# GpSimd's items of the last layer in chains of their own, given out at chosen steps, and the late transpositions of x at steps 7 and 8

## The chip, the cores and the metric

The kernel runs on one core of one Trainium2 chip. Its time is what the device takes for one execution, in microseconds (us); a kernel is judged by the median of several executions. A core has a tensor engine (PE, which loads weights on a second row of the profile, PEld), a vector engine (DVE), a scalar engine (ACT), GpSimd (POOL) and SyncE (SP), whose queue issues nearly all DMAs here. Each engine works through its own queue in order; semaphores tie them together.

## The reference

A small graph network over 16 sequences `b` of 1024 nodes with 128 features, all with one adjacency matrix. Three layers are multi-head attention with a feed-forward part, and one last layer is a graph attention with one head:

```
# layers 0, 1, 2 (8 heads of 16)
scores = einsum(Q, K) / sqrt(16);  attn = softmax(where(adj == 0, -inf, scores))
x = layer_norm(h + attn @ V @ Wo + bo)
x = layer_norm(x + relu(x @ W1 + b1) @ W2 + b2)
# last layer
h = x @ W;  e = leaky_relu(s_i[:, None] + s_j[None, :])      # s_i = h @ a_src, s_j = h @ a_dst
att = softmax(where(adj == 0, -inf, e));  out = layer_norm(att @ h + x) * gamma + beta
```

Everything is in float32.

## The kernel before, in words

**Blocks and steps.** The work is cut into 48 blocks `m`, one for each pair of a sequence and a layer 0 to 2. The sequences go in groups of four ("panels" below): blocks 0 to 11 are the three layers of sequences 0 to 3, blocks 12 to 23 those of sequences 4 to 7, and so on; within a panel all four do layer 0, then layer 1, then layer 2. A block has 32 steps, numbered 0 to 31; the running number of a step is `n`, so that step 4 of block 14 is n = 452. In a step, `score_step` makes the scores of 128 keys with 512 queries for four heads: PE makes two tiles of 128x1024 (L545), and each is masked and exponentiated. One of them goes by ACT (exp, L553) and then POOL (multiplication by a 0/1 mask, L554), the other by DVE (an added mask, L557) and then ACT (L569). At the ten steps of `BOTH_ON_DVE` (3, 7, 8, 15, 23, 24, 26, 28, 30, 31) both go by DVE, and POOL has no multiplication. Four steps later (`AHEAD`), `av_step` multiplies the result by V on PE (L574).

**Pieces.** All other work is cut into pieces that are given out between the steps: the projections of the next block (`proj_tasks`), what follows the attention of an earlier block (`post_tasks`), the transposition of the next `x` (`transpose_x`), and the last layer of a finished sequence (`last_tasks`). Pieces stand in chains. A task is `(gap, function, tiles)`: it is due `gap` steps after its predecessor in the chain. `piece` gives out at most one piece without a `*` in a step, and any number of those with one (those hold no work of PE). `need` takes pieces out of their chains at once, due or not, until a mark is done; it is called where the next block cannot start without something. In `tiles`, `+x` claims one of the five buffers for a sequence's `x`, `-x` gives it back; `w` and `last` are counted in the same way (8 and 2).

**What sets the order on the engines.** The order on PE, ACT and SP is the order of the program. POOL and DVE are ordered by the framework's scheduler, and `tc.issue_after(behind["pool"])` puts an item behind POOL's latest mask multiplication. A buffer is waited for where its new user stands, in that engine's queue.

**A panel's end.** When a sequence has finished layer 2, its last layer runs as pieces inside the blocks that follow. `xt` transposes x on PE, `nodes` makes h and the exponentials of the two scores, `rows_gh` and `send_rows` split these into rows and send them by 16 small DMAs on SP into `g_rows` and `h_rows` (L756, L757). Eight times, `edges(v)` makes the edge scores of 128 nodes on PE from those rows (L769), DVE masks them (L774), and `aggregate(v)` multiplies by h on PE (L383, 32 columns at a time), adds x on DVE and gathers the statistics of the final norm. After `aggregate(3)` and `aggregate(7)`, `normalise` works on half of the rows on POOL (L433 to L441). POOL multiplies x by the second norm's gain and adds its bias in place before that (`by_rows`, two of 128x1024), and multiplies and adds the last gain and bias afterwards (`by_rows` for each half, 128x512, all L798). `store` sends a half by four DMAs on SP. Only then is the buffer of x free, and `fetch` of a sequence of the next panel can claim it (eight DMAs on SP, L167). In a block whose `x` was fetched too late for the usual transposition by DMA, PE transposes it in two pieces with the mark `xP` (L345); their steps stand in `AT["xP"]`. `stack` (step 24 for the heads 0 to 3 of the next block, step 1 for the heads 4 to 7 of the running one) lays out Q and K with 16 DMAs on SP (L530).

**After the last step** the chains that are left are given out in turns until they are empty: the last layers of the sequences 13, 14 and 15 ("the tail" below).

Of the kernel before, what the change touches and what calls it, by code (L numbers as in the profile page):

```python
# [30 lines left out]
FIRST = 1  # L31


AT = {"xP": (4, 6), "proj": (5, 7, 9, 11, 17, 19), "post": (13, 15, 17, 18, 21, 22, 22, 23, 24, 25, 27, 29, 31, 35, 38, 40)}
AT_V_LAST = (9, 11, 17, 19, 20, 21)
AT_FIRST = (12, 14, 16, 18, 20, 22)
T_AT = 22
STACK_AT = 24
AT_END = {3: (12, 21, 22, 24, 25, 26, 27, 28, 30, 31), 2: (8, 9, 13, 14, 15, 16, 17, 18, 20, 21)}
AHEAD = 4  # L40
BOTH_ON_DVE = (3, 7, 8, 15, 23, 24, 26, 28, 30, 31)
TILES = {"w": 8, "x": LANES + 1, "last": 2}
BLOCKED = -57344.0
# [76 lines left out]
def fast_path(ctx: ExitStack, tc: tile.TileContext, a: dict, out: bass.AP, flag):  # L120
    nc = tc.nc
# [4 lines left out]
    L = 3  # L126
# [12 lines left out]
    def bank():  # L139

        if head[0] or tail[0]:
            return slot()[:, :512]
        return psum.tile([P, 512], F32, tag="t", name="t", bufs=1)
# [197 lines left out]
    def transpose_half(dst, src, h, gain=None, bias=None):  # L341

        ps = bank()
        for t in range(4):
            nc.tensor.transpose(ps[:, t * P:(t + 1) * P], src[:, 4 * h + t, :], identf)  # L345
        dv, pv = dst.rearrange("p (j t e) -> p t j e", j=4, t=4), ps.rearrange("p (t j e) -> p t j e", j=4, t=4)
        with soon():
            if gain is None:
                nc.scalar.copy(dv, pv)
            else:  # L350
                nc.scalar.activation(dv, pv, AF.Identity, scale=gain, bias=bias)
# [72 lines left out]
    def normalise(n, ts):  # L424

        scalars(n, ts)
        subtract_scale(n, ts)
# [68 lines left out]
    def transpose_x(m, by_dma=True):  # L496
        b, l = blocks[m]
        x, xT = state["x", b], xt_tile("xT")
        state["xT", m] = xT
        if by_dma:  # L500
            put(moved(lambda: xT, lambda: x), ("xT", m))
        elif m == 0:
            for h in range(2):
                transpose_half(xT[:, h], x, h)
        else:
            put([(0, lambda: transpose_half(xT[:, 0], x, 0), ""), (0, lambda: transpose_half(xT[:, 1], x, 1), "")],
                ("xP", m), first=True)

        def scale():
            with tc.issue_after(behind["pool"]) if m else nullcontext():  # L510
                nc.gpsimd.tensor_mul(x, x, rows(W[l - 1]["ln2_g"]))

        def shift():
            with tc.issue_after(behind["pool"]) if m else nullcontext():
                nc.gpsimd.tensor_add(x, x, rows(W[l]["bo"]))
        if m:
            put(([(6, scale, "*")] if l else []) + [(2 if l else 6, shift, "*")], ("shifted", m))
        else:
            shift()

# [180 lines left out]
    def last_tasks(b):  # L701
# [3 lines left out]
        def xt(h):  # L705
            def run():
                w = W[L - 1]
                if h == 0:

                    s["col"] = work.tile([P, 4, NT], F32, tag="col", name="col", bufs=2)  # L710
                    s["hd"] = [work.tile([P, 4, D + 1], F32, tag="w", name="hd", bufs=TILES["w"]) for _ in range(2)]
                    s["n"] = with_stats(state["x", b])
                s["xT", h] = half_tile("xT")
                transpose_half(s["xT", h], state["x", b], h, w["ln2_gc"], w["ln2_bc"])
            return run

        def nodes(t0, t1):
            def run():
                col, ts = s["col"], slice(t0, t1)

                halves = [slice(max(t0, 4 * h), min(t1, 4 * h + 4)) for h in range(2)]
                halves = [(c, s["hd"][c.start // 4][:, c.start % 4:(c.stop - 1) % 4 + 1, :])
                          for c in halves if c.start < c.stop]
                ps = bank()
                for t in range(t0, t1):
                    by_columns(ps[:, (t - t0) * (D + 2):(t - t0 + 1) * (D + 2)],
                               s["xT", t // 4][:, t % 4 * P:(t % 4 + 1) * P], w_nodes)
                pv = ps[:, :(t1 - t0) * (D + 2)].rearrange("p (t d) -> p t d", d=D + 2)
                with soon():
                    nc.scalar.activation(col[:, 2, ts], pv[:, :, D + 1], AF.Exp, scale=NEG_SLOPE)  # L730
                    nc.scalar.activation(col[:, 0:2, ts].rearrange("p c t -> p t c"), pv[:, :, D:], AF.Exp,
                                         scale=1 - NEG_SLOPE)
                    for c, hd in halves:
                        nc.vector.tensor_mul(hd[:, :, :D], pv[:, c.start - t0:c.stop - t0, :D],
                                             col[:, 2, c, None].to_broadcast([P, c.stop - c.start, D]))
                for c, hd in halves:
                    nc.scalar.copy(hd[:, :, D], col[:, 2, c])
            return run
# [22 lines left out]
        def edges(v):  # L761
# [14 lines left out]
                                                   1.0, mask01[:, :, q:q + SLOT], op0=OP.max, op1=OP.mult)  # L776
            return run

        def aggregate(v):
            def run():  # L780
                e, ps = s["e", v], bank()
                for t in range(NT):
                    by_columns(ps[:, :D + 1], e[:, t, :], s["hd"][t // 4][:, t % 4, :], start=(t == 0), stop=(t == NT - 1))
                nc.vector.reciprocal(s["col"][:, 3, v:v + 1], ps[:, D:D + 1])
                nc.vector.scalar_tensor_tensor(s["n"][0][:, v, :], ps[:, :D], s["col"][:, 3, v:v + 1],
                                               state["x", b][:, v, :], op0=OP.mult, op1=OP.add)
                stats(s["n"], slice(v, v + 1))
                if v % 4 == 3:
                    with tc.issue_after(behind["pool"]):
                        normalise(s["n"], slice(v - 3, v + 1))  # L790
                if v == NT - 1:
                    check_range(s["col"].rearrange("p c t -> p (c t)"))
            return run

        def by_rows(op, z, v, n=NT):
            def run():
                with tc.issue_after(behind["pool"]):
                    op(z(), z(), rows(v(), n))  # L798
            return run
# [16 lines left out]
        def two(f, g):  # L816
            def run():
# [1 line left out]
                g()  # L819
            return run  # L820

        mul, add = nc.gpsimd.tensor_mul, nc.gpsimd.tensor_add
        tasks = [(5, xt(0), "+w +last +w +w"), (1, xt(1), "+w"), (2, nodes(0, 3), ""), (2, nodes(3, 6), ""),
                 (0, by_rows(mul, x, lambda: W[L - 1]["ln2_g"]), "*"), (2, nodes(6, 8), "-w -w"),
                 (0, by_rows(add, x, lambda: ln2_b_last), "*"), (2, rows_gh, ""), (1, send_rows, "*"), (7, edges(0), "")]
        for v in range(NT - 1):
            tasks.append((2, two(edges(v + 1), aggregate(v)), ""))
            if v in (4, 6):
                tasks.append((0, by_rows((mul, add)[v // 2 - 2], y(0), lambda v=v: wl[("ln_gamma", "ln_beta")[v // 2 - 2]], 4), "*"))
        tasks += [(2, aggregate(NT - 1), ""), (2, store(0), "-last -w -w *"), (1, by_rows(mul, y(1), lambda: wl["ln_gamma"], 4), "*"),  # L830
                  (2, by_rows(add, y(1), lambda: wl["ln_beta"], 4), "*"), (3, store(1), "-x *")]
        return tasks


    blocks = [(b, l) for p in range(0, B, LANES) for l in range(L) for b in range(p, p + LANES)]
    chains = []
    done = {("fetch", b) for b in range(2)}
    now = [0]
    free = dict(TILES)
    free["x"] -= 2  # L840

    def put(tasks, mark, chain=None, first=False, table=None):

        if chain is None:
            chain = {"due": now[0], "queue": deque()}
            chains.insert(0 if first else len(chains), chain)
        for n, task in enumerate(tasks):
            at = now[0] // (4 * NT) * 4 * NT + (table or AT[mark[0]])[n] if mark[0] in AT else None
            chain["queue"].append(task + (mark if n == len(tasks) - 1 else None, at))
        return chain  # L850

    def take(chain):

        _, f, tiles, mark, _ = chain["queue"][0]
        if any(free[t[1:]] == 0 for t in tiles.split() if t[0] == "+"):
            return False
        chain["queue"].popleft()
        f()
        for t in tiles.replace("*", "").split():
            free[t[1:]] += -1 if t[0] == "+" else 1  # L860
        done.add(mark)
        chain["due"] = now[0]
        if not chain["queue"]:
            chains.remove(chain)
        return True

    def is_due(chain):
        gap, at = chain["queue"][0][0], chain["queue"][0][4]
        return now[0] >= max(chain["due"] + gap, at or 0)

    def piece():
# [371 lines left out]
```

## Time and profile before

| | |
|---|---|
| median of 3 runs | 3924.72 us (3922.28 to 3926.63) |
| profiled execution, its own time | 3922.55 us |
| its span in the profile | 3920.7 us |
| PE busy | 3715.7 us, 95% |
| POOL busy | 3477.6 us, 89% |
| DVE busy | 3460.5 us, 88% |
| ACT busy | 3296.9 us, 84% |
| issues of `h_rows` and `g_rows` on SP | 124 and 124 |
| score multiplications with the mask on POOL (L554) | 1056, 2029 ns each |
| a `by_rows` of 128x1024 and of 128x512 on POOL (L798) | 2392 ns and 1286 ns |

The span reaches from the first instruction to the last; some 2 us lie around it. A line of the timeline gives the start in us from the span's start, the duration, the engine and the source line, what is written and read, how many instructions are merged, and in brackets the idle time ahead of it and what ended it. "SPq" are DMA issues on SP. A line of the waits gives the waiting engine and line, the one that ended the wait, and the sum, the number and the longest of these waits. A line of the table by stage gives a stretch, its length, and the busy time of PE, PEld, DVE, ACT and POOL in it.

### The profile page before, as it was taken

To read this page: it belongs to the slowest core of one execution; us is meant where nothing else is said; L and a number is where in the kernel's file an instruction comes from. 1 tells how busy PE (TensorE), PEld (TensorE's weight loads), DVE (VectorE), ACT (ScalarE), POOL (GpSimd) and SP (SyncE) were. 2 spreads that over 40 slices of the span, in tenths; PEclk is the share of its full clock that TensorE was granted. 3 is DMA by queue.
4 is the path that set the end of the run, shared out by engine and by line. 5 is a ranking of instruction groups with operands and counts; after the bars stand their busy time and mean duration, and the time that the engine had idled before them with its cause. 6 is when DMAs were issued, how large, how long until landed. Compare 5 with 4: busy or idle time off the path is not lost.

```text
span 3920.7 us, 109674 instructions
## 1 busy us (share of the span) xinstructions
PE 3715.7 (95%) x44385; PEld 1515.1 (39%) x44385; DVE 3460.5 (88%) x5860; ACT 3296.9 (84%) x3797; POOL 3477.6 (89%) x2971
## 2 busy tenths in 40 slices
PE   7999999999989999999998999999999999999987
PEld 2333333344434333334443333333444433333346
DVE  6999999989878999998897899998898889999876
ACT  7989999977877999997777899999777789999850
POOL 5899999988978999998878899999887899999885
PEclk8999999999999999999999999999999999999998
DMA  5424334322323334332222324334232323424200
GB/s 139 113 73 103 91 81 110 76 70 70 89 63 79 98 72 110 80 95 73 72 67 76 92 66 101 95 74 100 73 82 52 88 71 93 103 71 106 63 8 21
DMA packets 245887, 319.28 MB, mean 81 GB/s; under 512 B 51072, under 2 KB 174208, under 8 KB 245376
## 3 DMA queue, kind: packets, MB, share of 16 engines
q1 hardware_dynamic: 243840, 311.52, 31.7%
q8 instruction: 353, 5.78, 0.6%
q14 instruction: 158, 1.29, 0.1%
q10 hardware_dynamic: 1536, 0.68, 0.1%
HBM read 58.53 MB, written 51.38 MB: 28 GB/s over the span
## 4 chain that ended last, share of the span: by engine, by line
POOL 46%; PE 38%; ACT 5%; DVE 5%; issue 3%; SPq 2%; DMA 1%; DVEq 0%; ACTq 0%; POOLq 0%
POOL e L554 27%; PE acc L574 13%; PE t L383 12%; PE s L545 9%; POOL x L441 7%; POOL mv L435 4%; POOL x L632 4%; ACT e L553 3%; DVE e L557 3%; ACT e L569 2%; PE s L769 2%; POOL x L798 2%; PE s L383 1%; POOL A L589 1%; SPq L530 1%
## 5 line engine op out<-in xcount | busy, mean ns | idle before, releaser
L557 DVE TENSOR_TENSOR e<-s,mask_add 128x1024 f32<-128x1024 f32 x2016 | 2377.4, 1211 | 240.3 <-PE s L545 214.5
L554 POOL TENSOR_TENSOR e<-e,mask 128x1024 f32<-128x1024 f32 x1056 | 2120.1, 2029 | 241.6 <-ACT e L553 227.8
L569 ACT ACTIVATE e<-e 128x1024 f32<-128x1024 f32 x2016 | 2110.9, 1062 | 185.2 <-DVE e L557 156.3
L574 PE MATMUL acc<-e,v 128*17 128x512 f32 x12288 | 1629.0, 602 | 78.6 <-POOL e L554 64.8
L553 ACT ACTIVATE e<-s 128x1024 f32<-128x1024 f32 x1056 | 1083.3, 1026 | 250.6 <-PE s L545 244.8
L545 PE MATMUL s<-Wq,Wk 64*128 64x512 f32 x6144 | 1196.4, 458 | 32.3 <-DVE e L557 21.1
L545 PEld LDWEIGHTS s<-Wq,Wk 64*128 64x128 f32 x6144 | 499.8, 185 | 1085.2 <-issue 388.9
L574 PEld LDWEIGHTS acc<-e,v 128*17 128x17 f32 x12288 | 205.2, 96 | 595.2 <-issue 351.1
L441 POOL TENSOR_SCALAR x<-x,mv 128x128 f32<-128x128 f32 x896 | 388.1, 448 | 19.1
L435 POOL TENSOR_TENSOR mv<-mv,half_neg 128x4 f32<-128x4 f32 (+1 forms) x179 | 214.0, 1195 | 13.6
L413 DVE BATCH_NORM_STATS2 st<-x 128x6 f32<-128x128 f32 x896 | 204.0, 281 | 7.7
L383 PE MATMUL t<-hd,ee 128*32 128x129 f32 x6656 | 205.7, 275 | 2.5 <-DVE x L420 2.4
L383 PE MATMUL t<-x1T,W 128*32 128x512 f32 x1520 | 201.9, 603 | 0.3
L774 DVE SCALAR_TENSOR_TENSOR ee<-s,mask 128x256 f32<-128x256 f32 x512 | 179.8, 413 | 23.4 <-PE s L769 23.4
L383 PEld LDWEIGHTS t<-W,hT 128*32 128x32 f32 x6080 | 170.9, 111 | 59.5 <-issue 48.4
L383 PEld LDWEIGHTS t<-hd,ee 128*32 128x32 f32 x6656 | 178.8, 110 | 16.1 <-DVE x L420 5.8
L383 PE MATMUL t<-W,hT 128*32 128x128 f32 x6080 | 184.7, 274 | 0.1
L589 POOL TENSOR_TENSOR A<-tt,recs 128x256 f32<-128x256 f32 x192 | 119.8, 624 | 49.7 <-DVE recs L588 49.6
L420 DVE TENSOR_TENSOR x<-t,x 128x512 f32<-128x512 f32 x191 | 129.1, 676 | 38.3 <-PE t L383 38.0
L649 ACT ACTIVATE hT<-t,b 128x512 f32<-128x512 f32 x190 | 130.4, 686 | 23.3 <-PE t L383 22.5
L585 DVE STREAM_TRANSPOSE tt<-acc 128x512 f32<-128x512 f32 x192 | 135.3, 705 | 0.0
L357 DVE STREAM_TRANSPOSE xb<-x 128x512 f32<-128x512 f32 x164 | 115.0, 701 | 20.1 <-POOL x L441 19.9
(145 smaller groups left out, 2531.1 us busy)
## 6 DMA issues: line engine op xcount, KB each, us to landing
Wk<-hi SPq DMA_DIRECT2D x384, 128.0 KB
Wk<-lo SPq DMA_DIRECT2D x384, 128.0 KB
Wq<-hi SPq DMA_DIRECT2D x384, 128.0 KB
Wq<-lo SPq DMA_DIRECT2D x384, 128.0 KB
tr<-xb SPq DMA_DIRECT2D x656, 64.0 KB
x1T<-tr SPq DMA_DIRECT2D x90, 256.0 KB
xT<-tr SPq DMA_DIRECT2D x74, 256.0 KB
x<-in_x_dram SPq DMA_DIRECT2D x124, 64.0 KB
```

The source lines that it names most:

```text
L383: nc.tensor.matmul(dst[j:j + SLOT, :], cols, rhs, start=start, stop=stop)
L413: nc.vector.bn_stats(st[:, t, :], z[:, t, :])
L435: nc.gpsimd.tensor_tensor(v, v, half_neg[:, ts], OP.pow)
L441: nc.gpsimd.tensor_scalar(z[:, t, :], z[:, t, :], mv[:, t, 0:1], mv[:, t, 1:2], op0=OP.add, op1=OP.mult)
L545: nc.tensor.matmul(ps[:, r * 512:(r + 1) * 512], k[64 * r:64 * r + 64, kt * P:(kt + 1) * P], q[64 * r:64 * r + 64, q0:q0 + 512], start=Tru ...
L553: nc.scalar.activation(ev, psv, AF.Exp, scale=HD ** -0.5)
L554: behind["pool"] = nc.gpsimd.tensor_mul(ev, ev, m).ins
L557: behind["dve"] = nc.vector.tensor_add(ev, psv, m).ins
L569: nc.scalar.activation(ev, ev, AF.Exp, scale=HD ** -0.5)
L574: nc.tensor.matmul(acc[j * SLOT:j * SLOT + HD + 1, :], v_bufs[m % 2][:, kt, 2 * j + g, :], e[:, j, :], start=first, stop=last)
L589: nc.gpsimd.tensor_mul(state["A"][:, qh, :, g, :], tt[:, :, :HD], rec[:, :, None].to_broadcast([P, 16, HD]))
L774: nc.vector.scalar_tensor_tensor(e[:, :, j * SLOT:(j + 1) * SLOT], ps.rearrange("p (k q) -> p k q", q=P)[:, :, j * SLOT:(j + 1) * SLOT], 1 ...
```

## The change

The items of POOL in the last layer leave the chain of the last layer. The two `by_rows` that scale x form a chain `("scaled", b)`, started by `xt(1)`; `aggregate` calls for it if it isn't done. `normalise`, the two `by_rows` of a half and its `store` form a chain `("out", b, h)`, started by `aggregate(3)` and continued by `aggregate(7)`. Tasks with a `~` are given out only at the steps of `POOL_FREE`, and two steps apart at the least, as long as no `need` takes them. The buffer of x and the count `last` are given back by the second `store`, the two `w` by `aggregate(7)`. `xP` moves from the steps 4 and 6 to 7 and 8, and `shift` of a layer 0 (adding a bias to x on POOL, 128x1024) from 6 to 10 steps after its chain's start.

```
-AT = {"xP": (4, 6), "proj": (5, 7, 9, 11, 17, 19), "post": (13, 15, 17, 18, 21, 22, 22, 23, 24, 25, 27, 29, 31, 35, 38, 40)}
+AT = {"xP": (7, 8), "proj": (5, 7, 9, 11, 17, 19), "post": (13, 15, 17, 18, 21, 22, 22, 23, 24, 25, 27, 29, 31, 35, 38, 40)}
+POOL_FREE = (0, 1, 2, 3, 4, 5, 6, 22, 23, 29, 30, 31)
...
-            put(([(6, scale, "*")] if l else []) + [(2 if l else 6, shift, "*")], ("shifted", m))
+            put(([(6, scale, "*")] if l else []) + [(2 if l else 10, shift, "*")], ("shifted", m))
...
                 transpose_half(s["xT", h], state["x", b], h, w["ln2_gc"], w["ln2_bc"])
+                if h == 1:
+                    put([(1, by_rows(mul, x, lambda: W[L - 1]["ln2_g"]), "*~"),
+                         (2, by_rows(add, x, lambda: ln2_b_last), "*~")], ("scaled", b), first=True)
...
+        def norm(h):
+            def run():
+                with tc.issue_after(behind["pool"]):
+                    normalise(s["n"], slice(4 * h, 4 * h + 4))
+            return run
         def aggregate(v):
             def run():
+                need_if(("scaled", b))
...
                 if v % 4 == 3:
-                    with tc.issue_after(behind["pool"]):
-                        normalise(s["n"], slice(v - 3, v + 1))
+                    s["out"] = put([(1, norm(v // 4), "*~"), (2, by_rows(mul, y(v // 4), lambda: wl["ln_gamma"], 4), "*~"),
+                         (1, by_rows(add, y(v // 4), lambda: wl["ln_beta"], 4), "*~"),
+                         (2, store(v // 4), "-x -last *" if v == NT - 1 else "*")], ("out", b, v // 4),
+                                   s["out"] if any(c is s.get("out") for c in chains) else None, first=True)
...
-                 (0, by_rows(mul, x, lambda: W[L - 1]["ln2_g"]), "*"), (2, nodes(6, 8), "-w -w"),
-                 (0, by_rows(add, x, lambda: ln2_b_last), "*"), (2, rows_gh, ""), (1, send_rows, "*"), (7, edges(0), "")]
+                 (2, nodes(6, 8), "-w -w"), (2, rows_gh, ""), (1, send_rows, "*"), (7, edges(0), "")]
         for v in range(NT - 1):
             tasks.append((2, two(edges(v + 1), aggregate(v)), ""))
-            if v in (4, 6):
-                tasks.append((0, by_rows((mul, add)[v // 2 - 2], y(0), lambda v=v: wl[("ln_gamma", "ln_beta")[v // 2 - 2]], 4), "*"))
-        tasks += [(2, aggregate(NT - 1), ""), (2, store(0), "-last -w -w *"), (1, by_rows(mul, y(1), lambda: wl["ln_gamma"], 4), "*"),
-                  (2, by_rows(add, y(1), lambda: wl["ln_beta"], 4), "*"), (3, store(1), "-x *")]
+        tasks.append((2, aggregate(NT - 1), "-w -w"))
...
     def take(chain):
...
+        if "~" in tiles:
+            pool_at[0] = now[0]
...
     def is_due(chain):
-        gap, at = chain["queue"][0][0], chain["queue"][0][4]
+        gap, tiles, at = chain["queue"][0][0], chain["queue"][0][2], chain["queue"][0][4]
+        if "~" in tiles and not tail[0] and (now[0] % (4 * NT) not in POOL_FREE or now[0] < pool_at[0] + 2):
+            return False
         return now[0] >= max(chain["due"] + gap, at or 0)
```

More of the change, by code (lines that the diff above doesn't have):

```diff
@@ L777, in edges @@
             return run
+        mul, add = nc.gpsimd.tensor_mul, nc.gpsimd.tensor_add
+        def norm(h):
[3 more added lines that the diff above has]
+            return run
         def aggregate(v):
             def run():
+                need_if(("scaled", b))
                 e, ps = s["e", v], bank()
@@ L820, in two @@
             return run
-        mul, add = nc.gpsimd.tensor_mul, nc.gpsimd.tensor_add
         tasks = [(5, xt(0), "+w +last +w +w"), (1, xt(1), "+w"), (2, nodes(0, 3), ""), (2, nodes(3, 6), ""),
-                 (0, by_rows(mul, x, lambda: W[L - 1]["ln2_g"]), "*"), (2, nodes(6, 8), "-w -w"),
-                 (0, by_rows(add, x, lambda: ln2_b_last), "*"), (2, rows_gh, ""), (1, send_rows, "*"), (7, edges(0), "")]
+                 (2, nodes(6, 8), "-w -w"), (2, rows_gh, ""), (1, send_rows, "*"), (7, edges(0), "")]
         for v in range(NT - 1):
             tasks.append((2, two(edges(v + 1), aggregate(v)), ""))
-            if v in (4, 6):
-                tasks.append((0, by_rows((mul, add)[v // 2 - 2], y(0), lambda v=v: wl[("ln_gamma", "ln_beta")[v // 2 - 2]], 4), "*"))
-        tasks += [(2, aggregate(NT - 1), ""), (2, store(0), "-last -w -w *"), (1, by_rows(mul, y(1), lambda: wl["ln_gamma"], 4), "*"),
-                  (2, by_rows(add, y(1), lambda: wl["ln_beta"], 4), "*"), (3, store(1), "-x *")]
+        tasks.append((2, aggregate(NT - 1), "-w -w"))
         return tasks
@@ L837, in fast_path @@
     done = {("fetch", b) for b in range(2)}
-    now = [0]
+    now, pool_at = [0], [0]
     free = dict(TILES)
@@ L858, in take @@
         f()
-        for t in tiles.replace("*", "").split():
+        if "~" in tiles:
+            pool_at[0] = now[0]
+        for t in tiles.replace("*", "").replace("~", "").split():
             free[t[1:]] += -1 if t[0] == "+" else 1
```

## The prediction

> **What bounds the kernel now.** I read the page's busy times first, then the busy times by stage, PE's waits in each stage, and the timelines of PE, POOL and SP where they differ.
>
> ```profile
> PE 3715.7 (95%) x44385; PEld 1515.1 (39%) x44385; DVE 3460.5 (88%) x5860; ACT 3296.9 (84%) x3797; POOL 3477.6 (89%) x2971
> ```
>
> PE is occupied nearly always, and the change leaves its work alone. So the change can only remove or add idle time of PE. The table by stage (a usual block, then 13 and 14) shows where that is:
>
> ```profile
> 392.10:462.50 70.40, 68.53 (x713) 24.14 (x707) 65.44 (x99) 67.18 (x75) 67.62 (x56) 1.00 0.39 92
> 1005.76:1098.15 92.39, 90.15 (x1333) 43.41 (x1329) 84.11 (x170) 70.26 (x85) 75.66 (x65) 1.00 0.25 66
> 1098.15:1196.31 98.16, 85.00 (x1086) 37.05 (x1083) 76.62 (x136) 71.56 (x89) 80.47 (x68) 0.97 0.30 78
> ```
>
> Block 14 idles for 13.2 us, the others for about 2. Its longest wait, and the tail's:
>
> ```profile
> 1117.58 1.08 PE L345 MATMUL t<-identf,x 128*128 128x128 f32 x4 [7.80 <-DMA x<-in_x_dram]
> 3857.55 1.08 PE L769 MATMUL s<-g_rows,h_rows 4*128 4x128 f32 x7 [5.21 <-DMA h_rows<-parts]
> ```
>
> The transposition of step 4 waits for a late `fetch`. PE's waits over the whole span have three of these, one for each panel but the last:
>
> ```profile
> PE t L345 <- DMA x<-in_x_dram: 21.0, 3, 7.8
> ```
>
> SP's timeline says why, in block 14 and then in block 13:
>
> ```profile
> 1090.31 20.66 SPq L812 DMA_DIRECT2D out_dram<-x  x8
> 1112.47 3.66 SPq L167 DMA_DIRECT2D x<-in_x_dram  x8
> ```
>
> ```profile
> 1002.47 4.81 SPq L167 DMA_DIRECT2D x<-in_x_dram  x8
> 1007.39 0.48 SPq L530 DMA_DIRECT2D Wk<-hi  x1
> ...
> 1016.79 1.23 SPq L530 DMA_DIRECT2D Wq<-lo  x2
> 1020.36 0.71 SPq L756 DMA_DIRECT2D g_rows<-parts  x1
> ...
> 1030.47 0.60 SPq L757 DMA_DIRECT2D h_rows<-parts  x1
> ```
>
> SP is one queue: `store`, `fetch`, `stack` (16 DMAs, 10.7 us) and `send_rows` (16 DMAs, 10.7 us) follow each other. In block 13 all of them are early enough: rows are usable about 1.5 us after the last issue (in block 23 it ended at 1780.2 and PE, waiting, went on at 1781.70), here at 1032.6, and the first `edges` needs them at 1038.78.
>
> ```profile
> 999.83 2.03 POOL L554 TENSOR_TENSOR e<-e,mask 128x1024 f32<-128x1024 f32 x1
> 1106.93 1.29 POOL L798 TENSOR_TENSOR x<-x,ln_beta 128x512 f32<-128x512 f32 x1
> ```
>
> From POOL's timeline: step 29's multiplication in block 12, and the last item of POOL ahead of block 14's `fetch`. It ends at 1108.2; the last store is issued 2.75 us later, `fetch` runs from 1112.47 to 1116.13, and PE uses x at 1117.58: 9.4 us from POOL's end to x, 7.9 to the end of `fetch` on SP.
>
> [...] nothing passes the 20.66 us above. [...] after 7.80 us of waiting four transpositions took 1.08 us instead of 0.66. Steps 4 to 7 of blocks 14, 26 and 38 last 18.5, 18.6 and 17.9 us against 9.2 in all for the same work (2.25 and 2.5 for steps 4 and 5 when they don't wait, then 2.2 and 2.3): a wait of 7 us costs 9.1 with its clock.
>
> **The change, part by part** (t = 0 is a block's first score; step lengths are distances of L545 in PE's timeline). From the order in which the changed program stands:
>
> *Block 14: -9.1 us.* `aggregate(7)` comes two steps earlier. Its PE work ends at about t = -3.5, DVE's statistics 2.2 us later, POOL's normalisation (3.5) and two `by_rows` (1.29 each, 1.36 with the gap) end at 4.9, and x is there at 14.3. The transpositions, now at steps 7 and 8, need it at 18. No wait remains.
>
> *Blocks 12 and 13: a burst.* The restriction to `POOL_FREE` leaves the items undone until block 12 (and 13) starts; there `need` for the next `fetch` takes all that is left, behind step 29's multiplication and ahead of step 0's. In block 12 this is a `by_rows` of x (2.39), two normalisations (3.5 each) and four halves (1.36 each): 14.8 us. Step 29's multiplication ends at -4.3, so the burst ends at 10.5 and step 0's multiplication at 12.5. PE wants that at step 4, t = 9.3: a wait of 3.2 us, +4 with some clock. The products of steps 1 and 2 follow at 14.5 and 16.5, and steps 5 and 6 ask at about 15 and 17, so they add little. x lands at 19.9, and step 7 asks at about 21.6. Behind `fetch` on SP stands `stack` for heads 4 to 7; it leaves at 10.5 + 7.9 + 10.7 = 29.1, and step 16 wants it at some 50: hidden. `send_rows` of this sequence went out before the burst, at step 29 of block 11.
>
> In block 13 it is two `by_rows` of x, one normalisation and four halves: 2.40 + 2.39 + 3.5 + 5.4 = 13.7 us from -5.0 to 8.7. `fetch` leaves SP at 8.7 + 7.9 = 16.6, 15 us later than today (1007.3, t = 1.5). Queued behind it are `stack` (to 27.4) and `send_rows` (to 38.2); the rows land at 39.7. Before, the first `edges` stood at step 14; it now stands at step 12, because `nodes` and `rows_gh` no longer make way for `xP`. The twelve steps last 27.2 us and `edges` comes 1.7 into its step: 28.9. PE waits 10.8 us in all (part of it already at step 0's product and at step 7 for x, at 18.1). With 2.1 for the clock, and 0.8 less for a wait at the block's end that `aggregate` no longer meets: +12.1.
>
> *Block 11, step 29: -3.3 us.* It lasts 5.1, 6.1 and 6.4 us in the panels, 2.8 without its wait for POOL; with step 30 that gives 2.3, 3.9 and 3.6. 11.7 us of POOL items leave the steps before it. The like wait in block 10 goes too, but its 2.3 to 3.9 us gain nothing: `edges(0)` at block 11's step 0 already waits for rows (2.0 us at 1781.70; at 822.77 it starts as they land), so PE only comes earlier to a queue that isn't faster.
>
> *Block 15: -2 us*: part of its idle excess over a usual block (1.4, 3.6 and 4.4), what waits for POOL.
>
> Sum for a panel: -9.1 + 4 + 12.1 - 3.3 - 2 = +1.7, three times +5. The later `shift` costs nothing: step 10 lies in stretches where PE paces the steps; at step 0 of blocks 1, 2 and 11 its 2.4 us fit before step 4.
>
> *Tail: +7 us.* In block 47 a 2.4 us wait for POOL goes, but 7.4 us of `by_rows` now stand between the last multiplication and the `by_rows` that the last feed-forward sum needs; the product `A` ends at 3815.8 instead of 3815.4, so this is even. Then SP: the first `store` of sequence 13 now stands ahead of `send_rows` of sequence 14. Its data need the fourth `aggregate` of sequence 13 (its PE work ends at 3842.1), POOL's two items for sequence 14 and a normalisation that stand ahead (to 3844.9), then a normalisation and two halves: ready at about 3851.1, gone from SP at 3853.5; 10.7 for the rows and 1.5 to land give 3865.8 instead of 3857.55: +8.2. The rows of sequence 15 get one more `aggregate` as cover: -1.1.
>
> Total +12.4 on the profiled execution's 3922.55 (span 3920.7, which I raise alike). That execution is 2.2 below the median of the runs, 3924.72, so I expect 3935 to 3937: **3936**.
>
> **Rivals.** *The rows are in time, so it is faster.* If `edges(0)` of block 13 finds its rows, all three panels lose 36 us less: 3912 by clearing two thirds of it, 3900 for all. For it: SP's chain is a sum of five parts that I take from other blocks, and POOL could reach the burst earlier than its multiplication of step 29 lets me think. Against it: `stack` takes 10.4 to 11.9 us wherever I look, `send_rows` 10.7 to 11.0, and POOL has nothing that it could put ahead. It decides at the lateness: below some 6.7 us instead of 10.8 the whole change gains. *The tail hides its store:* `norm` of sequence 13 done earlier, +5 in all, 3929; against it: that input, and what stands ahead of it on POOL. *POOL is later than I count:* the burst starts late or the blocks 14 and 15, where I find margins below 1 us, add waits: +4 a panel and more, 3950. *The change does nothing:* excluded, the orders on POOL, PE and SP differ.
>
> **How the numbers follow.** As computed 0.48 (own range 3925 to 3947), rows in time 0.24, tail hidden 0.15, POOL later 0.13. 0.2% (7.8 us) is about what a measurement tells from no change. Slower: 0.41 of the first, all of the last, a little of the third: 0.56. Faster: the rival and a bit of the first: 0.25. The range 3902 to 3952 takes in two fifths of the faster case.
>
> **What would show it.** Right: PE's L769 waits for `h_rows` or `g_rows` by about 10 us at step 12 of blocks 13, 25 and 37 and by about 12 in the tail; no L345 waits for x at block 14; L574 waits 3 us for POOL at step 4 of block 12. Wrong: `send_rows` of block 13 leaving SP before t = 30, or any of POOL's burst given out before step 29.

## The result, and the profile after

The changed kernel takes 3962.06 us (median of 4 runs, 3958.66 to 3964.19) against 3924.69 us before: a ratio of 1.0095 (1.0077 to 1.0112), slower. The forecast was 3936 with a range of 3902 to 3952: the direction is right, the loss is three times as large. The profiled span grew from 3920.7 to 3960.6 us.

Lines of the changed kernel lie some further down than before: scores L546, products with V L575, mask on POOL L555, `edges` L773, transposition L346, `fetch` L168, `store` L827. The busy times of the page after:

```profile
PE 3730.7 (94%) x44385; PEld 1519.2 (38%) x44385; DVE 3464.9 (87%) x5860; ACT 3295.5 (83%) x3797; POOL 3478.6 (88%) x2971
```

Each engine does the same work. PE is busy 15 us longer with as many instructions; more of them run at half clock (a granted clock of 0.50 in the trace, as from 1056.66 to 1061 us behind a wait of 4.70 us; the mean over the span is 0.978, and 0.983 before). The rest of the 40 us is idle time. The busy times by stage, for the blocks 12, 13 and 14:

```profile
919.12:1017.40 98.28, 93.37 (x1324) 44.07 (x1321) 82.71 (x164) 69.90 (x82) 82.40 (x78) 0.97 0.26 67
1017.40:1120.17 102.77, 92.40 (x1333) 44.49 (x1329) 83.59 (x167) 70.41 (x85) 80.95 (x77) 0.95 0.25 66
1120.17:1208.63 88.46, 83.10 (x1085) 36.14 (x1081) 77.27 (x140) 71.28 (x89) 79.58 (x66) 1.00 0.34 86
```

Block 14 is 9.7 us shorter than before, block 13 10.4 us longer, and block 12, where the forecast had 4, is 7.8 us longer. PE's waits show the exchange, first those of the kernel before for the rows and for `lo`, then those of the changed kernel:

```profile
PE t L383 <- DVE lo L473: 9.7, 6, 1.7
PE s L769 <- DMA h_rows<-parts: 6.3, 3, 5.2
...
PE s L769 <- DMA g_rows<-parts: 2.0, 1, 2.0
```

```profile
PE acc L575 <- POOL e L555: 64.3, 127, 3.6
PE s L773 <- DMA h_rows<-parts: 31.7, 7, 4.9
PE t L384 <- DVE lo L474: 18.0, 12, 2.2
PE s L773 <- DMA g_rows<-parts: 16.3, 4, 8.1
...
PE t L346 <- DMA x<-in_x_dram: 0.2, 1, 0.2
```

The 21.0 us for x have shrunk to 0.2; the waits for the rows grew from 8.3 to 48.0 us, and those for this `lo` on DVE (what `hi` leaves of a projection in layer 0) from 9.7 to 18.0, of which 6.6 are new waits at step 10 of blocks 12, 24 and 36. Block 13 shows what was forecast. SP's timeline, then PE's:

```profile
1020.66 8.10 SPq L827 DMA_DIRECT2D out_dram<-x  x8
1030.14 4.50 SPq L168 DMA_DIRECT2D x<-in_x_dram  x8
1034.74 0.48 SPq L531 DMA_DIRECT2D Wk<-hi  x1
...
1044.90 0.70 SPq L760 DMA_DIRECT2D g_rows<-parts  x1
...
1054.94 0.60 SPq L761 DMA_DIRECT2D h_rows<-parts  x1
```

```profile
1051.52 0.44 PE L773 MATMUL s<-g_rows,h_rows 4*128 4x128 f32 x1 [2.62 <-DMA g_rows<-parts]
1056.66 1.08 PE L773 MATMUL s<-g_rows,h_rows 4*128 4x128 f32 x7 [4.70 <-DMA h_rows<-parts]
```

`fetch` leaves SP 17.2 us into the block (forecast 16.6), the rows 38.1 (38.2), and PE goes on at 39.3 (39.7). It waits in two pieces, because the first of eight products needs fewer rows: 7.3 us in all (8.1 and 7.2 in blocks 25 and 37), where the prediction named about 10. The two other waits that it named are there too: 13 us for the rows in the tail (about 12 named), and 2.6 us for POOL at step 4 of block 12 (3 named).

The table gives the length of stages less that of the kernel before, in us, from the distances of the first score products; each sum is over the three panels. "Forecast" is the prediction's own working. Every column is one profiled execution, and not all are from one chip; the kernel before took 3923 to 3931 us on the chips of the experiments. The ratios below are each against it on the same chip, and they decide; the table says where.

| | forecast | after | e1 | e2 | e5 | e6 | e7 | e8 |
|---|---|---|---|---|---|---|---|---|
| block 2 | 0 | +5.2 | +0.1 | +4.2 | +5.1 | +0.2 | +0.1 | +4.4 |
| blocks 10, 11 | -9.9 | -3.5 | +0.9 | +0.3 | -1.0 | +0.5 | -4.1 | +2.1 |
| block 12 | +12 | +23.6 | +14.4 | +13.0 | +13.1 | 0.0 | +32.0 | +3.8 |
| block 13 | +36.3 | +34.6 | +13.8 | -7.9 | -6.7 | -6.7 | +26.7 | -6.7 |
| block 14 | -27.3 | -28.6 | -12.9 | -28.6 | -27.8 | -21.2 | -11.3 | -28.4 |
| block 15 | -6 | -1.7 | +0.2 | +0.4 | +0.4 | -0.5 | -0.2 | +0.1 |
| block 47 and tail | +7 | +11.5 | +2.1 | +9.3 | +3.2 | +1.5 | +10.7 | +0.9 |
| whole span | +12.4 | +39.9 | +20.2 | -8.0 | -12.1 | -24.8 | +55.9 | -24.1 |

### The profile page after: what moved, and what is told of

Read it like the earlier page. It is cut to its first block, busy times and chain, and to the rows that moved or that the text cites. A ratio compares the mean times of both kernels' runs of the same rounds, so it can differ in the third digit from the quotient of the medians.

```text
span 3960.6 us, 109707 instructions
## 1 busy us (share of the span) xinstructions
PE 3730.7 (94%) x44385; PEld 1519.2 (38%) x44385; DVE 3464.9 (87%) x5860; ACT 3295.5 (83%) x3797; POOL 3478.6 (88%) x2971
## 4 chain that ended last, share of the span: by engine, by line
POOL 46%; PE 37%; ACT 6%; DVE 3%; SPq 3%; issue 3%; DMA 2%; ACTq 0%; POOLq 0%; DVEq 0%
POOL e L555 27%; PE acc L575 13%; PE t L384 12%; PE s L546 9%; POOL x L442 7%; POOL mv L436 4%; POOL x L633 4%; ACT e L554 3%; ACT e L570 2%; POOL x L813 2%; PE s L773 2%; DVE e L558 2%; PE s L384 1%; SPq L531 1%; POOL A L590 1%
## 5 line engine op out<-in xcount | busy, mean ns | idle before, releaser
L555 POOL TENSOR_TENSOR e<-e,mask 128x1024 f32<-128x1024 f32 x1056 | 2119.1, 2027 | 284.4 <-ACT e L554 282.4
L575 PE MATMUL acc<-e,v 128*17 128x512 f32 x12288 | 1631.7, 603 | 73.6 <-POOL e L555 64.3
L546 PE MATMUL s<-Wq,Wk 64*128 64x512 f32 x6144 | 1201.0, 460 | 28.9 <-DVE e L558 15.6
L546 PEld LDWEIGHTS s<-Wq,Wk 64*128 64x128 f32 x6144 | 501.0, 186 | 1080.9 <-issue 386.7
L575 PEld LDWEIGHTS acc<-e,v 128*17 128x17 f32 x12288 | 204.7, 95 | 593.2 <-issue 354.3
L590 POOL TENSOR_TENSOR A<-tt,recs 128x256 f32<-128x256 f32 x192 | 119.6, 623 | 39.3 <-DVE recs L589 39.2
L650 ACT ACTIVATE hT<-t,b 128x512 f32<-128x512 f32 x190 | 130.4, 686 | 15.3 <-PE t L384 14.4
L773 PE MATMUL s<-g_rows,h_rows 4*128 4x128 f32 x1024 | 92.1, 296 | 48.3 <-DMA h_rows<-parts 31.7
```

Source lines behind the costliest of these rows:

```text
L546: nc.tensor.matmul(ps[:, r * 512:(r + 1) * 512], k[64 * r:64 * r + 64, kt * P:(kt + 1) * P], q[64 * r:64 * r + 64, q0:q0 + 512], start=Tru ...
L555: behind["pool"] = nc.gpsimd.tensor_mul(ev, ev, m).ins
L575: nc.tensor.matmul(acc[j * SLOT:j * SLOT + HD + 1, :], v_bufs[m % 2][:, kt, 2 * j + g, :], e[:, j, :], start=first, stop=last)
L773: nc.tensor.matmul(ps[:, r * 512 + k * P:r * 512 + (k + 1) * P], h_rows[row, k * P:(k + 1) * P], g_rows[row, half].rearrange("p (j q) -> p ...
```

## The experiments

**e1: the late transpositions alone, and what they need.**

```
# against the kernel before
-AT = {"xP": (4, 6), ...
+AT = {"xP": (7, 8), ...
```

> The kernel before with the late transpositions of x alone (xP at steps 7 and 8); POOL's items stay in the old chain and are given out as they fall due. Theory (the gain and the loss of the change are separable, and the loss is all in the chains): PE's wait for x at step 4 of blocks 14, 26 and 38 goes with its half clock, about 9.5 us each; the wait of 0.8 us at the end of blocks 13, 25 and 37 goes too, 2 to 3 us with its clock; nothing is added. 3924.7 - 3 x 12 = 3889, at most 3897 if block 13 keeps its wait. Rival (the late transpositions cost something by themselves: K's projection at step 9 follows them directly and rows_gh moves up a step): waits appear at steps 9 to 11 of blocks 12 to 14 and eat most of it, 3910 or more.

Measured: 1.0032 (1.0019 to 1.0045), slower: the rival's number, but mostly not for the rival's reason. Of its waits at steps 9 to 11 there is one that is new, at step 10 of block 12 (see e8); the larger ones are at the transposition itself. PE's timeline in block 14, and POOL's:

```profile
1134.68 1.11 PE L345 MATMUL t<-identf,x 128*128 128x128 f32 x4 [7.00 <-POOL x L515]
```

```profile
1132.28 2.35 POOL L515 TENSOR_TENSOR x<-x,bo 128x1024 f32<-128x1024 f32 x1
```

L515 is `shift`. It writes x in place, was given out at step 6, and so came before the transposition at step 7, which now had to wait for it. So e1 transposes x with the bias already added, and no longer computes the same thing: its time shows the order, not a price that the late transpositions must have. The two edits of the diff's first half belong together: moving `shift` behind step 8 is what makes `xP` at 7 and 8 possible.

**e2: own chains, all steps free.**

```
# against the changed kernel
-POOL_FREE = (0, 1, 2, 3, 4, 5, 6, 22, 23, 29, 30, 31)
+POOL_FREE = range(32)
```

> The changed kernel with its own chains and its two-step spacing, but POOL_FREE holding all 32 steps. Theory (the restriction to twelve steps makes the burst in front of fetch, and the burst makes the waits): at the start of blocks 12 and 13 nothing but the store and fetch is left, so L575's wait at step 4 of block 12, the wait at step 10 behind it and the wait for g_rows and h_rows at step 12 of block 13 all go. Block 12 loses 7.9 us against the changed kernel, block 13 10 to 13 us, so 55 to 65 us in all: 3895 to 3907; block 2's 5 us and the tail's stay. Rival (own chains and the spacing are the cost, whichever steps are free): rows still come late, 3940 or more.

Measured: 0.9968 (0.9960 to 0.9976) against 1.0095 of the changed kernel, about 50 us less by the ratios and 48.0 by the spans: below the 55 expected, and far from the rival. One list of steps decides between faster and slower. L575's wait at step 4 of block 12 and both of L773's in block 13 are gone, and block 13 is 42.5 us shorter in sum. Block 12 loses only 10.6 of its 23.6 us: 4.3 us a panel are there without the burst.

**e3: the rows ahead of `stack`.**

```
# against the changed kernel
-                if at == (6 if m == 0 else 1):
+                if at == (6 if m == 0 else 12 if m % 12 == 1 and m > 1 else 1):
                     stack(m, 1)
```

> The changed kernel with stack for heads 4 to 7 of blocks 13, 25 and 37 given out at step 12 instead of 1, so that send_rows stands ahead of it on SP; POOL's burst is untouched. Theory (the rows of block 13 are late because they queue behind stack's 10.2 us on SP): send_rows then leaves as soon as fetch has, about 17.4 us into the block instead of 27.5, the rows are usable at about 29.3 and edges(0) asks at about 30.5; both waits of L773 there (7.3 us) go with their half clock. 9 to 11 us for each of three blocks: 3929 to 3935. stack then ends at about 39, and step 16 asks for it at some 45: no new wait. Rival (the rows are late by their own data, or edges waits for something else): no change, 3960 to 3964; rival (stack becomes the late one): a wait of L546 at step 16 takes the gain.

Measured: 1.0097 (1.0080 to 1.0114), no gain. The rows did leave at 1035.8 to 1046.5, right behind `fetch`, and no L773 waits in block 13. The second rival was right that `stack` takes the gain, but at step 11, not 16. ACT's timeline and PE's:

```profile
1056.02 0.58 ACT L473 CAST hi<-t 128x512 fp32r<-128x512 f32 x1 [13.35 <-DMA Wk<-hi]
```

```profile
1057.49 1.93 PE L384 MATMUL t<-xT,Wk 128*32 128x512 f32 x8 [11.64 <-DVE lo L474]
```

The next block's `hi` and `lo` go into the buffers that `stack` reads (`hl`, four of them), and their first projection stands at step 9. So `stack` is wanted there and the rows at step 12, each with 16 DMAs in one queue: 10.2 us for `stack` and 10.7 for the rows here. With `fetch` ending 17 us into the block, one of the two is late in either order. An earlier `fetch`, as in e2, takes both waits away; sending one of the two from another engine's queue was not tried.

**e4: the tail's first store behind the rows.**

```
# against the changed kernel, in aggregate
-                         (2, store(v // 4), ...
+                         (3 if b == B - 3 and v < NT - 1 else 2, store(v // 4), ...
```

> The changed kernel with a gap of 3 instead of 2 ahead of the first store of sequence 13, which puts it behind send_rows of sequence 14 on SP. Theory (in the tail SP waits for that store's data): the rows' parts are there at 3878.5 and SP sends them at 3884.0, so about 5.5 us are won, no more, because the parts themselves come 4.8 us later than before: 3956 to 3957, and L773 still waits about 7.5 us in all. Rival (the tail is held by POOL or by sequence 15): within 2 us of the changed kernel.

Measured: 1.0084 (1.0067 to 1.0100). The interval overlaps that of the changed kernel, so the times alone don't show the 5.5 us; what follows is read from one profiled execution of each. SP's timeline in the tail, first of the changed kernel, then of e4:

```profile
3848.66 35.26 SPq L827 DMA_DIRECT2D out_dram<-x  x8
3884.02 0.65 SPq L760 DMA_DIRECT2D g_rows<-parts  x1
```

```profile
3849.82 1.76 SPq L827 DMA_DIRECT2D out_dram<-x  x4
3879.21 0.64 SPq L760 DMA_DIRECT2D g_rows<-parts  x1
```

From block 47's start to PE's last product, the changed kernel takes 9.3 us more than the kernel before and e4 3.5: these 5.8 us were SP waiting for the store's data. The other 3.5 are not settled: counted from block 47's start, the rows' parts are ready 4.8 us later than before, and one more pair of `edges` and `aggregate` (2.6 us) stands ahead of `rows_gh` on PE, but that pair is work which doesn't come again.

**e5: both edits of the first half.**

```
# against the kernel before
-AT = {"xP": (4, 6), ...
+AT = {"xP": (7, 8), ...
-... [(2 if l else 6, shift, "*")], ("shifted", m))
+... [(2 if l else 10, shift, "*")], ("shifted", m))
```

> The kernel before with both moves of the diff's first half, xP at steps 7 and 8 and shift at a gap of 10, and none of the chains. In e1 the transpositions of blocks 13 and 14 waited at step 7 for POOL's shift (L345 <- POOL x L515, 5.1 and 7.0 us), which adds bo to the same x in place and stood ahead of them at step 6; e1 thus also transposed x with bo already added, which is a change of what it computes. Theory (that order alone made e1 slow; the burst of the chains makes the rest of the change's loss): no L345 waits at step 7; block 14 loses 9.8 us against the kernel before, block 13 2.6, block 12 keeps the 4.4 us that e1 and e2 show, from a wait for lo at step 10; block 2 pays 1 to 5 us. 3 x -8 + 3: ratio about 0.9945, 21 us less. Rival (POOL is late in blocks 13 and 14 whatever stands there, and only own chains keep it clear): L345 still waits 3 us or more at step 7 for x, ratio 1.000 or above.

Measured: 0.9958 (0.9945 to 0.9972), faster; no L345 waits at step 7, as the theory has it. The changed kernel without its chains is a gain, of 17 us where 21 were expected. The table's other entries are near what was expected, with the 4.4 us of block 12 among them, 3.8 of these at the steps 10 and 11. e2, which has the chains with every step free, is at 0.9968, and the two intervals overlap: no run here shows that the chains gain anything.

**e6: the same in two blocks of a panel only.**

```
# against the kernel before
-                ("xP", m), first=True)
+                ("xP", m), first=True, table=(7, 8) if m % 12 in (2, 3) else None)
-... [(2 if l else 6, shift, "*")], ("shifted", m))
+... [(2 if l else 10 if m % 12 in (2, 3) and not by_dma else 6, shift, "*")], ("shifted", m))
```

> The kernel before with xP at steps 7 and 8 and shift at 10 only where block 13 or 14 of a panel transposes for the next (blocks 13, 14, 25, 26, 37, 38); everywhere else as before. Theory (block 12's 4.4 us come from its own late transpositions, block 2's loss from shift at step 0): both vanish, block 13 still wins 2.6 and block 14 9.8 us. 3 x -12.2: ratio about 0.9907, 36 us less. Rival (block 12's wait at step 10 comes from elsewhere, as the edges' steps): it stays, ratio about 0.994.

Measured: 0.9920 (0.9907 to 0.9934), 3897.7 us against 3930.1 before on that chip: the lowest ratio here, ahead of both kernels (its interval overlaps that of e8). Block 12 and block 2 are back at their old lengths. In two panels block 14 loses 3.4 us at the steps 20 and 21, in the third it doesn't. In block 14 itself PE runs at half clock there: behind a wait of 0.85 us, scores take 1.22 us instead of 0.73 and products with V 1.91 instead of 1.05.

**e7: the chains alone.**

```
# against the changed kernel
-AT = {"xP": (7, 8), ...
+AT = {"xP": (4, 6), ...
-... [(2 if l else 10, shift, "*")], ("shifted", m))
+... [(2 if l else 6, shift, "*")], ("shifted", m))
```

> The changed kernel with xP back at steps 4 and 6 and shift back at 6: the chains and the twelve steps alone. Theory (the burst delays fetch, and x is then what step 4 waits for): x lands about 20 us into block 12 and 18 us into block 13 and is wanted at about 9, so L345 waits about 10 us in each at step 4; the rows of block 13 then come in the shadow of that wait. Blocks 12 and 13 together cost at least as much as in the changed kernel, block 14 keeps a wait of some 5 us, the tail's 11 us stay: ratio 1.010 to 1.018. Rival (the chains are harmless without the late transpositions): ratio below 1.004.

Measured: 1.0111 (1.0096 to 1.0127). The waits for x are there, but 4.1 to 6.2 us in blocks 12 and 13 where 10 were expected; in part because 2.7 us in block 12 and 1.4 in block 13 had already been lost to POOL a little earlier in the step. In block 14, with the transposition back at step 4, 6.4 to 7.5 us stay. PE's timeline in block 12:

```profile
934.41 1.09 PE L346 MATMUL t<-identf,x 128*128 128x128 f32 x4 [5.45 <-DMA x<-in_x_dram]
```

In sum the halves of the change nearly add: the stages of the table come to -13.7 us for e5, +53.9 for e7 and +41.1 for the changed kernel. Part of that is chance. Stage by stage they do not add (block 13: -6.7 and +26.7 against +34.6; block 12: +13.1 and +32.0 against +23.6), and e7's profiled execution is the slowest of its four; by the ratios, 0.42% won and 1.11% lost make 0.7% against the 0.95% measured. The form of the loss differs: with the early transpositions it is x that comes late behind the burst, with the late ones it is the rows.

**e8: what makes block 12 long.**

```
# against e5, in edges: around the loop that issues DVE's four products
+                with tc.issue_after(low[now[0] - 1]) if now[0] - 1 in low and not tail[0] else nullcontext():
```

> e5 with one order added: DVE takes the products of edges only after lo of the step before. It swaps two neighbours in DVE's order three times, in blocks 12, 24 and 36 at step 10, and moves nothing else. Theory (block 12's own loss is PE at step 10 waiting for its one bank t, which lo of step 9 must empty first, and lo stands behind edges on DVE): the wait of 2.20 us of L383 <- DVE lo goes, step 10 lasts 4.6 instead of 8.4 us or so, block 12 comes to about 91 us instead of 94.8; 11 us less than e5, ratio about 0.993. Rival (lo is late by its own input, DVE's backlog after the transposed A): the wait stays at 1 us or more, ratio about 0.9955.

Measured: 0.9938 (0.9925 to 0.9952). The interval overlaps e5's, so the effect is read from the traces: 3.1 us less than e5 in block 12 of every panel. Step 10 of block 12 in e5, DVE's timeline and then PE's:

```profile
948.70 1.42 DVE L774 SCALAR_TENSOR_TENSOR ee<-s,mask 128x256 f32<-128x256 f32 x4
950.04 0.68 DVE L473 TENSOR_TENSOR lo<-t,hi 128x512 fp32r<-128x512 f32 x1
```

```profile
950.86 2.83 PE L383 MATMUL t<-hd,ee 128*32 128x129 f32 x64 [2.20 <-DVE lo L473]
953.62 1.22 PE L545 MATMUL s<-Wq,Wk 64*128 64x512 f32 x4
```

and PE's in e8:

```profile
948.25 1.98 PE L383 MATMUL t<-hd,ee 128*32 128x129 f32 x64 [0.66 <-DVE lo L473]
950.16 0.73 PE L545 MATMUL s<-Wq,Wk 64*128 64x512 f32 x4
```

`aggregate` writes bank `t`, of which there is one; `lo` of step 9 must empty it first. The scheduler had put `lo` behind four products of `edges` (1.4 us), which PE had only just supplied. Putting it ahead takes 1.54 us off the wait, and with it the half clock: 2.83 becomes 1.98, and 1.22 becomes 0.73. The 0.66 us that stay are DVE's backlog. In the kernel before, `lo` stood ahead, and PE did not wait for it there. The late transpositions alone move it: e1 has the same wait of 2.20 us. That the cause is the projection at step 9, which now follows directly on them, is likely but not tested.

The changed kernel has the wait too, but not the half clock:

```profile
952.98 1.98 PE L384 MATMUL t<-hd,ee 128*32 128x129 f32 x64 [2.21 <-DVE lo L474]
954.89 0.73 PE L546 MATMUL s<-Wq,Wk 64*128 64x512 f32 x4
```

It is the same in blocks 24 and 36. The steps 10 and 11 therefore lose 2.3 us there, against 3.8 to 3.9 in e5 and e2 and 0.7 in e8.

## Why the prediction was wrong

**Right, in mechanism and size.** *Block 14* (-9.1 forecast, -9.7, -9.8 and -9.1 measured); it is the late transpositions' gain, since e5 has it without the chains (-9.2, -9.6 and -9.0) and e7, with the chains alone, mostly has not (-3.5, -4.8 and -3.0). *Block 13, the burst* (+12.1; +10.4, +12.0 and +12.2): SP's times agree to 0.7 us, e2 shows that the restriction makes it, e3 that SP's queue passes it on. The wait of 0.8 us at its end was undervalued: with its clock the two last steps gain 3.5. So the burst itself cost 13.0 to 14.9 us (the changed kernel less e2) where 12.9 were forecast, and the sum is as close as it is because two misses partly cancel. *Block 12, the burst itself* (+4): the wait at step 4 is 2.62 us where 3.2 were forecast; with its half clock (0.52 granted from 931.06 to 936 us) the steps 4 to 8 lose 5.0 to 5.1 us more than in e2.

**Wrong: "the transpositions, now at steps 7 and 8" were given a gain in block 14 and no price in block 12.** The step moved PE's pieces in three blocks, and I followed SP and POOL behind them but not DVE's order. It costs 4.3 to 4.4 us in block 12 with all steps free or without the chains (e2, e5), 3.1 of it through `lo` behind `edges` (e8). In the changed kernel, where PE kept its clock at that wait, `lo` costs 2.3. Over three panels block 12 is 11.6 us longer than forecast, the largest part missing: 6.8 are this wait, 3.2 the burst, which cost 5.1 a panel instead of 4, and the rest small shifts of other steps.

**Wrong: "the later `shift` costs nothing", with step 0 of block 2 among the places named.** There its 2.4 us do fit before step 4, as I said, but POOL then runs late up to the steps 12 and 13, where DVE scales the weights of layer 1. Timelines of the changed kernel: POOL, DVE and PE.

```profile
206.58 4.00 POOL L555 TENSOR_TENSOR e<-e,mask 128x1024 f32<-128x1024 f32 x2
210.78 2.01 POOL L555 TENSOR_TENSOR e<-e,mask 128x1024 f32<-128x1024 f32 x1 [0.20 <-ACT e L554]
```

```profile
206.78 3.94 DVE L303 TENSOR_SCALAR W<-W,ln_gc 128x256 f32<-128x256 f32 x1
210.65 0.27 DVE L305 TENSOR_SCALAR Wq<-Wq,ln_gc 128x128 f32<-128x128 f32 x1
210.85 2.02 DVE L305 TENSOR_SCALAR Wk<-Wk,ln_gc 128x128 f32<-128x128 f32 x1
```

```profile
214.98 0.79 PE L313 MATMUL t<-Wo,bvs 128*128 128x128 f32 x2 [4.21 <-DVE x L421]
```

In the kernel before the same two took 0.84 and 0.27 us. They end as POOL's multiplications end, at 210.6 and 212.8. Why they last so much longer, 3.94 us for 0.84 and 2.02 for 0.27, is not shown here, only that they end within 0.2 us of POOL's multiplications (the 0.84 us too). How much it costs differs from run to run: 0.8 to 5.2 us in the six runs with the later `shift` everywhere, 0.1 and 0.2 in e1, e6 and e7. e6 takes it away by leaving `shift` alone outside two blocks.

**Too large: "block 11, step 29: -3.3 us".** Blocks 10 and 11 together win 3.5 us in three panels where I had 9.9. That block 10's gain would be given back at block 11's step 0 was right, but it is given back with a surcharge: the wait for the rows there is 3.64 to 4.88 us, and the steps 0 to 2 lose 4.8, 2.8 and 7.0 us against the 3.9, 2.3 and 3.9 won. Step 29 itself won 1.5 to 2.7.

**Too large: "block 15: -2 us".** The waits at the steps 19 to 22 went, but `normalise` of sequence 3, held back until step 22, stands ahead of step 25's multiplication, and L575 waits 3.6 us at step 29, which is the longest of its kind in the list above. Net -0.5 a panel.

**Too small: "the tail: +7 us".** 11.5, of which e4 puts 5.8 on SP. The forecast's chain (store of sequence 13, then the rows) is the right one; the rows land 1.9 us later than I had, since POOL's two `by_rows` of sequence 14, which stand ahead of that store's own items, wait for a transposition that PE reaches only at 3866.2. From PE's last product to the end another 2.2 us were added (14.2 against 12.0), which e4 and e7 show too (1.9 and 2.5), e2 and e3 do not, and I can't explain.

The missing 11.6 + 5.2 + 6.4 + 4.3 + 4.5 us less small overestimates (3 us in blocks 13 and 14, 1.5 elsewhere) make up the 27.5 between +12.4 and +39.9.

## What to carry to other kernels

When pieces move between steps, follow every engine whose order a scheduler decides, not only the queues that the edit names: here one swap of neighbours on DVE was worth 3 us a panel, and one list of allowed steps about 50 us. Work that is held back for quiet steps is not saved; if something needs it, it comes in a burst in front of that need, and all that is queued behind (`fetch`, `stack`, the rows) inherits the delay. Before an item is moved in time, ask what reads or writes the same buffer in place: `xP` late is only possible with `shift` later still.

## What was not expected of the hardware

- The same DVE operation, `W` in block 2, took 0.84 us in the kernel before and 7.27 us in e2, with POOL busy beside it both times. In e2 it lasted from 205.08 to 212.35, while POOL worked through the end of one multiplication, a short product and three more multiplications without a pause, until 212.20. In e4 it took 1.58 us and ended at 208.69, about where the first of two multiplications ended; these two took 4.06 us together there and 4.00 in the changed kernel, where `W` ended behind the second (POOL's times are rough).
- PE's half clock came behind shorter waits than the 7.80 us that the prediction shows, and not every time. A wait of 2.20 us at step 10 of block 12 in e5 was followed by products that took 2.83 us instead of 1.98; waits of 2.20 and 2.21 us at step 10 of blocks 12, 24 and 36 in the changed kernel left them at 1.98 in all three. In the kernel before, a wait of 1.75 us at step 19 of block 15 was followed by score products of 1.07 and 1.22 us instead of 0.73, while blocks 27 and 39 kept 0.74 and 0.73 after 1.70 and 1.75 us. So the length of a pause alone doesn't decide it in these traces, and what does is left open. With the same wait of 2.2 us, step 10 of block 12 is 2.3 us longer than before in the changed kernel and 3.1 in e5.
